# Three small moves in a four-layer image kernel: weight sums to GpSimd, statistics to another loop, a residual to ScalarE and GpSimd

## The chip, the cores and the metric

The kernel runs on one core of a Trainium2 chip. The metric is the device time of one execution in microseconds, the median of five runs. The core's engines are named as the profile names them: PE (TensorE, matmuls; PEld are its weight loads), DVE (VectorE), ACT (ScalarE), POOL (GpSimd) and SP (SyncE, which issues DMAs). L12 is line 12 of the kernel before.

## The reference

Eight images x of 512 channels by 32 x 32 pixels, in float32, go through four layers. Cut to what matters:

```python
# layer 0: group norm (8 groups), attention with 8 heads, three inner steps, projection
h = group_norm(x, scale, bias)
q, k, v = split(qkv_w @ h + qkv_b)
h = softmax(q.T k / 8) v                      # per head, 64 channels
for _ in range(3):
    h = h + 0.1 * tanh(inl_w @ h + inl_b)
x = x + proj_w @ h + proj_b
# layer 1: attention with one head of 64 channels for q and k, 512 for v
x = x + (Wv x + bv) softmax(q.T k).T
# layer 2: upsample by 2 with a 12-tap FIR, leaky relu, downsample by 2
x = down(leaky_relu(up(x + bias)) * sqrt(2))
# layer 3: a bottleneck whose weights are mixed from 8 experts for each image
rw = sigmoid(mean(x) @ router_w.T + router_b)
w1, w2, w3 = (sum(rw[e] * w[e] for e in range(8)) for w in (w1, w2, w3))
h = relu(bn(conv1x1(x, w1)))                  # 512 -> 128 channels
h = relu(bn(conv3x3(h, w2)))                  # 128 -> 128
x = relu(bn(conv1x1(h, w3)) + x)              # 128 -> 512
```

## The kernel before, in words

Channels lie on partitions in four blocks of 128; an image is a tile of 128 partitions by 4 x 1024. Layers 0, 1 and 2 run image by image, and the result of each image is spilled to device memory. Layer 3 then runs over all images. The instructions of each engine are put into a fixed order when the program is built, and the pools of buffers decide which tile waits for which: a step on an engine waits for everything ahead of it on that engine.

**Products.** The 512 x 512 projections (q, k, v, inl, proj, and v of layer 1) are computed as seven products of quarter matrices instead of eight (`product`). This needs sums of quarters of the weights (five for each matrix, `weight`, L339 to L343) and of the data (eight operations for each source, `quarter_sums`, L353 to L356; their tiles are named T_h, T_hf and T_x). The product's steps are named P1, C11 (both in the banks `_A`, from plain quarters of the data and of the weight), U2, U3, C21 (banks `_X`) and C22, C12 (banks `_Y`); of these U2, U3, C21 and C22 read data sums, and U2, U3, C22 and C12 read weight sums. For image 0 the weight quarters are loaded from the inputs, two of them into a tile `raw_`, and the five sums are made, for q on DVE and for k and v on POOL; POOL's queue then stores the seven parts (`stored`), and later images load them ready-made.

**Group norm.** `group_norm` takes the statistics of x (L278, L279: eight `bn_stats` and four `bn_aggr`), averages over groups with two tiny matmuls (gn_mean, gn_var) and writes h. In the program's text it stands at the head of layer 0. In the built order the statistics of image b+1, whose x is loaded early, run on DVE within the v product of layer 1 of image b.

**Layer 0's projection.** The residual x + proj is partly added by POOL (L523, three adds of the P1 term for each of two u), beside DVE's T_hf.

**Layer 1.** The v product is interleaved with the scores. Then a loop over eight blocks ic of 128 positions (the AV loop, L722 on) transposes x (xT), adds row_bias on DVE into a tile `y` (two buffers), multiplies by the attention, finishes y on DVE (L737), and writes it by DMA to a padded image, from which `halo` loads read overlapping tiles for layer 2.

**Layer 3.** `mixed(b)` forms the mixed weights of image b in a tile of two buffers, in five parts (w1e, three of w2e, w3e): each part is one product with the first expert's weight (L925) and seven multiply-adds (L927) on DVE. For image b, `c1` is a 1x1 product of z (16 matmul records), which ACT turns into `rim` (relu, batch norm, L942, one for each half g); `c2` is the 3x3 convolution of rim (36 records), which ACT turns into h2 (L958); `c3` is the last product (16 records, through two banks), whose eight results DVE scales and adds to z in place (L967), and ACT finishes with a relu (L970). In the built order, the c3 matmuls of image b alternate with c1 of image b+1.

Of the kernel before, what the change touches and what calls it, by code (L numbers as in the profile page):

```python
# [9 lines left out]
F32 = mybir.dt.float32  # L10
BF16 = mybir.dt.bfloat16
AF = mybir.ActivationFunctionType  # L12
ALU = mybir.AluOpType
# [4 lines left out]
P = 128  # L18
B, C, H, W = 8, 512, 32, 32
S = H * W  # L20
CC = C // P
# [31 lines left out]
def tile_sequence(ctx: ExitStack, tc: tile.TileContext, a: dict, out: bass.AP, shifted: bool):  # L53
# [213 lines left out]
                    ps[r], ones[HD * r : HD * r + 1, :], shift[r], start=False, stop=True  # L267
                )

    def group_norm(b, x):  # L270

        stats = tmp(f"stats_{b}", S)[:, 0 : CC * 2 * 6].rearrange(
            "p (c h s) -> p c h s", c=CC, h=2
        )
        mv = small.tile([P, CC, 2], F32, tag="mv", bufs=2, name=f"mv_{b}")
        for cc in range(CC):
            for h in range(2):
                nc.vector.bn_stats(stats[:, cc, h, :], x[:, cc, ts(h, HALF)])  # L278
            nc.vector.bn_aggr(mv[:, cc, :], stats[:, cc, :, :].rearrange("p h s -> p (h s)"))  # L279
        mean_c, var_c = mv[:, :, 0], mv[:, :, 1]  # L280
        ps = bank(ps_tp, f"gn_mean_{b}")
        nc.tensor.matmul(ps[:, 0:CC], group_mean, mean_c, start=True, stop=True)
        mean = small.tile([P, CC], F32, tag="gmean", bufs=2, name=f"gmean_{b}")
        nc.vector.tensor_copy(mean, ps[:, 0:CC])
        dev = small.tile([P, CC], F32, tag="gdev", bufs=2, name=f"gdev_{b}")
        nc.vector.tensor_sub(dev, mean_c, mean)
        nc.vector.tensor_mul(dev, dev, dev)
        nc.vector.tensor_add(dev, dev, var_c)
        ps = bank(ps_tp, f"gn_var_{b}")
        nc.tensor.matmul(ps[:, 0:CC], group_mean, dev, start=True, stop=True)  # L290
        mul = small.tile([P, CC], F32, tag="gmul", bufs=2, name=f"gmul_{b}")
        nc.scalar.activation(mul, ps[:, 0:CC], AF.Sqrt, bias=eps)
        nc.vector.reciprocal(mul, mul)
        nc.vector.tensor_mul(mul, mul, gn_scale)
        add = small.tile([P, CC], F32, tag="gadd", bufs=2, name=f"gadd_{b}")
        nc.vector.tensor_mul(add, mean, mul)
        nc.vector.tensor_sub(add, gn_bias, add)
        h = big_tile(f"h_{b}", [P, CC, S])
        for cc in range(CC):
            nc.vector.tensor_scalar(  # L300
                h[:, cc, :], x[:, cc, :], mul[:, cc : cc + 1], add[:, cc : cc + 1],
                ALU.mult, ALU.add,
            )
        return h
# [19 lines left out]
    def weight(key, b):  # L324
        t = wpool.tile([P, len(PARTS), 2, QR], F32, tag="w", name=f"w_{key}_{b}", bufs=3)
        if b:
            nc.sync.dma_start(t, stored[key])
            return t
        src = a["qkv_wT"][:, "qkv".index(key) * C :] if key in "qkv" else a[key + "_wT"]
        raw = tmp(f"raw_{key}", S).rearrange("p (a cc o) -> p a cc o", a=2, o=QR)  # L330
        a21, a22 = raw[:, 0], raw[:, 1]
        for dst, i, j in ((t[:, 0], 0, 0), (t[:, 1], 0, 1), (a21, 1, 0), (a22, 1, 1)):
            nc.sync.dma_start(
                dst, src[j * QR : j * QR + QR, i * QR : i * QR + QR].rearrange(
                    "(cc p) o -> p cc o", p=P
                )
            )
        eng = nc.vector if key == "q" else nc.gpsimd
        eng.tensor_add(t[:, 3], a21, a22)  # L339
        eng.tensor_sub(t[:, 4], t[:, 3], t[:, 0])  # L340
        eng.tensor_sub(t[:, 5], t[:, 0], a21)
        eng.tensor_sub(t[:, 6], t[:, 1], t[:, 4])
        eng.tensor_scalar(t[:, 2], a22, -1.0, None, ALU.mult)  # L343
        nc.gpsimd.dma_start(stored[key], t)
        return t

# [186 lines left out]

        return made

    def layer0(b, x, w):
        h = group_norm(b, x)
        t = quarter_sums(f"h_{b}", h)
        q = big_tile(f"q_{b}", [P, CC, S])
        k = big_tile(f"k_{b}", [P, CC, S])  # L540
# [92 lines left out]
        if b + 1 < B:  # L633
            w["k"] = weight("k", b + 1)

    def layer1(b, x, w):

        qk = big_tile(f"qk1_{b}", [P, S + HALF])
        q, k = qk[:, 0:S], qk[:, S : S + HALF].rearrange("d (p j) -> d p j", j=P)
# [82 lines left out]
        for ic in range(SC):  # L722
            ps = bank(ps_tp, f"xT_{b}_{ic}")
            for cc in range(CC):
                nc.tensor.transpose(ps[:, ts(cc, P)], x[:, cc, ts(ic, P)], ident)
            y = work.tile([P, C], F32, tag="y", name=f"y_{b}_{ic}", bufs=2)
            nc.vector.tensor_add(y, ps, row_bias)
            ps = bank(name=f"av1_{b}_{ic}")
            sh, u = divmod(ic, 4)
            for jc in range(SC):  # L730
                nc.tensor.matmul(  # L731
                    ps, eT[sh][:, jc, ts(u, P)], v[:, jc, :],
                    start=(jc == 0), stop=(jc == SC - 1),
                )
            if ic == 1:
                totals(1)
            nc.vector.scalar_tensor_tensor(y, ps, inv[:, ic : ic + 1], y, ALU.mult, ALU.add)  # L737
            for r in range(4):
                nc.scalar.dma_start(
                    ypad[b % 2][4 * ic + r + 3, 3 : W + 3, :], y[W * r : W * r + W, :]  # L740
                )
            if ic:
                halo.load(ic - 1)
        halo.load(NT - 1)
        halo.load_last()
        return halo
# [96 lines left out]
    with tc.tile_pool(name=f"weights_{run}", bufs=1) as wpool:  # L843
        w = {key: weight(key, 0) for key in ("q", "k", "v")}
        w["qk1"] = wpool.tile([P, CC, P], F32, name="w_qk1")
        for i, key in enumerate(("q1_wT", "k1_wT")):
            nc.sync.dma_start(
                w["qk1"][:, :, ts(i, HD)], a[key].rearrange("(cc p) o -> p cc o", p=P)
            )

        for b in range(B):
            x = x_next
            layer0(b, x, w)
            if b + 1 < B:
                x_next = load_x(b + 1)
            halo = layer1(b, x, w)
            layer2(b, halo)


# [58 lines left out]
    def mixed(b):  # L918
        wt = pool3.tile([P, WCOLS], F32, tag="mixed", name=f"mixed_{b}")
        parts = [(w1e, 0, C)]  # L920
        parts += [(w2e[ky], C + ky * 3 * P, 3 * P) for ky in range(3)]
        parts += [(w3e, C + 9 * P, C)]
        for src, at, n in parts:
            dst = wt[:, at : at + n]
            nc.vector.tensor_scalar_mul(dst, src[:, 0, :], rw[:, b, 0:1])  # L925
            for e in range(1, NE):
                nc.vector.scalar_tensor_tensor(  # L927
                    dst, src[:, e, :], rw[:, b, e : e + 1], dst, ALU.mult, ALU.add
                )
        return wt  # L930

    wt_next = mixed(0)
    for b in range(B):
        z, wt = z_next, wt_next
        if b + 1 < B:
            z_next = load_z(b + 1)
            wt_next = mixed(b + 1)
        h1 = rims[b % 2]
        for g in range(2):
            ps = bank(name=f"c1_{b}_{g}")  # L940
            project(ps, wt[:, 0:C].rearrange("p (cc o) -> p cc o", o=P), 0, z, g)
            nc.scalar.activation(  # L942
                h1[:, 1 + 16 * g : 17 + 16 * g, 1 : W + 1],
                ps.rearrange("p (h w) -> p h w", w=W),
                AF.Relu, bias=bn[0][1], scale=bn[0][0],
            )
        h2 = pool3.tile([P, S], F32, tag="h2", name=f"h2_{b}")
        for g in range(2):
            ps = bank(name=f"c2_{b}_{g}")
            for tap in range(9):  # L950
                ky, kx = divmod(tap, 3)
                nc.tensor.matmul(  # L952
                    ps.rearrange("p (h w) -> p h w", w=W),
                    wt[:, C + tap * P : C + (tap + 1) * P],
                    h1[:, ky + 16 * g : ky + 16 * g + 16, kx : kx + W],
                    start=(tap == 0), stop=(tap == 8),
                )
            nc.scalar.activation(  # L958
                h2[:, ts(g, HALF)], ps, AF.Relu, bias=bn[1][1], scale=bn[1][0]
            )  # L960
        for oc in range(CC):
            for g in range(2):
                ps = bank(ps_tp, f"c3_{b}_{oc}_{g}")
                at = C + 9 * P + oc * P
                nc.tensor.matmul(ps, wt[:, at : at + P], h2[:, ts(g, HALF)], start=True, stop=True)
                dst = z[:, oc, ts(g, HALF)]
                nc.vector.scalar_tensor_tensor(  # L967
                    dst, ps, bn[2][0][:, oc : oc + 1], dst, ALU.mult, ALU.add
                )
                nc.scalar.activation(dst, dst, AF.Relu, bias=bn[2][1][:, oc : oc + 1])  # L970
            nc.sync.dma_start(out[b, ts(oc, P), :], z[:, oc, :])

    if shifted:
# [80 lines left out]
```

## Time and profile before

| | |
|---|---|
| median of five runs | 4117.13 us (4112.2 to 4117.71) |
| profiled execution: time, span | 4118.64 us, 4116.4 us |
| granted TensorE clock over the span | 0.988 |
| busy over the span: PE, DVE, ACT, POOL | 97%, 59%, 26%, 13% |
| first matmul (gn_mean of image 0) | 28.70 us |
| PE's idle before proj_X, 16 times | 41.0 us |
| first matmul of layer 3's c1 | 3867.56 us |

Times are microseconds from the start of the span. The timeline's lines give start, duration, engine, line, operation, `out<-in`, the number of instructions that are merged, and in brackets the idle time before them with what ended it. The groups' lines give busy time, mean duration in ns, and the idle time before them. "PE x <- DVE y" among the waits is time in which PE stood idle until DVE's y was done. The table of windows gives for each stretch the busy time of PE, PEld, DVE, ACT and POOL with the number of their instructions, then the granted clock, the share of DMA, and GB/s.

### The profile page before, as it was taken

The numbers are of one execution on the slowest core, as the hardware profiler recorded it, in microseconds if no ns is written. First come the engines' busy times: TensorE is split into PE (matmuls) and PEld (weight loads), VectorE is DVE, ScalarE is ACT, GpSimd is POOL, SyncE is SP. The second block draws the span as 40 slices with busy tenths as digits, with TensorE's granted clock in tenths as the row PEclk, the third lists the DMA queues.
The fourth block names the chain that finished last, engine by engine and source line by source line (L and its number), as shares of the span: only waits on it lengthen the run. The fifth ranks groups of instructions, "written<-read, shape, count | busy, mean of one in ns | idle before, by whom it ended". The sixth has DMA issues, their size and how long they took to land.

```text
span 4116.4 us, 36926 instructions
## 1 busy us (share of the span) xinstructions
PE 3977.3 (97%) x14034; PEld 1923.2 (47%) x14034; DVE 2443.4 (59%) x3421; ACT 1080.3 (26%) x1478; POOL 521.1 (13%) x382
## 2 busy tenths in 40 slices
PE   6999999999999999999999999999999999999899
PEld 3334553355434463355434554355533554345543
DVE  4768448634676347754486346763477345763696
ACT  0431214112332114212241123322142123422123
POOL 3321003100121002110030002110031001201000
PEclk9999999999999999999999999999999999999899
DMA  4002310032001310023101310013100221003333
GB/s 176 24 16 77 111 64 1 39 100 78 36 1 56 121 57 19 1 92 106 54 1 56 105 55 36 1 71 112 69 1 39 83 79 52 1 0 115 147 153 124
DMA packets 85307, 259.98 MB, mean 63 GB/s; under 512 B 13958, under 2 KB 20102, under 8 KB 78336
## 3 DMA queue, kind: packets, MB, share of 16 engines
q1 hardware_dynamic: 69520, 227.31, 15.5%
q10 hardware_dynamic: 12960, 16.81, 1.5%
q0 software_dynamic: 2640, 13.40, 0.9%
q8 instruction: 113, 1.85, 0.2%
q14 instruction: 74, 0.61, 0.0%
HBM read 194.57 MB, written 62.91 MB: 63 GB/s over the span
## 4 chain that ended last, share of the span: by engine, by line
PE 84%; DVE 11%; ACT 2%; issue 1%; DMA 0%; SPq 0%; ACTq 0%; DVEq 0%
PE scores L263 12%; PE av L731 11%; PE av L595 10%; PE inl_X L389 6%; PE dn L819 6%; PE v_X L389 4%; PE inl_A L389 4%; PE inl_Y L389 4%; DVE up L778 3%; PE v_Y L389 3%; PE c L952 3%; PE proj_X L389 2%; PE q_X L389 2%; PE k_X L389 2%; PE v_A L389 2%; ACT leak L777 2%
## 5 line engine op out<-in xcount | busy, mean ns | idle before, releaser
L580 ACT ACTIVATE e<-scores 128x1024 f32<-128x1024 f32 x512 | 496.7, 1022 | 506.7 <-PE scores L263 504.2
L586 DVE TENSOR_TENSOR acc<-acc,e 128x1024 f32<-128x1024 f32 x384 | 493.7, 1286 | 116.3 <-ACT e L580 97.8
L263 PE MATMUL scores<-q,k 64*128 64x512 f32 x2048 | 511.3, 616 | 9.9 <-ACT e L580 6.6
L595 PE MATMUL av<-e,v 128*64 128x512 f32 x2048 | 494.1, 604 | 0.0
L731 PE MATMUL av<-v,eT 128*128 128x512 f32 x1024 | 450.1, 592 | 0.0
L612 POOL TENSOR_TENSOR seen<-seen,acc 128x512 f32<-128x512 f32 x128 | 206.9, 1616 | 1607.9 <-DVE acc L586 1602.9
L263 PEld LDWEIGHTS scores<-q,k 64*128 64x128 f32 x2048 | 175.2, 186 | 338.1 <-ACT e L580 167.2
L777 ACT ACTIVATE leak<-up 128x512 f32<-128x512 f32 (+1 forms) x264 | 147.9, 595 | 591.5 <-DMA ypad_u<-y 445.0
L731 PEld LDWEIGHTS av<-v,eT 128*128 128x128 f32 x1024 | 189.6, 190 | 214.3 <-issue 212.1
L595 PEld LDWEIGHTS av<-e,v 128*64 128x64 f32 x2048 | 124.9, 136 | 338.8 <-issue 336.5
L389 PE MATMUL inl_X<-T_hf,w_inl 128*128 128x512 f32 x576 | 262.0, 592 | 0.0
L737 DVE SCALAR_TENSOR_TENSOR y<-av,inv,y 128x512 f32<-128x512 f32 x64 | 48.0, 750 | 360.2 <-PE av L731 360.2
L819 PE MATMUL dn<-dn_op,up 128*128 128x126 f32 (+5 forms) x2048 | 235.8, 275 | 0.0
L819 PEld LDWEIGHTS dn<-dn_op,up 128*128 128x128 f32 (+1 forms) x2048 | 231.1, 192 | 8.8 <-DVE up L778 6.5
L793 PE MATMUL up<-halo,up_op 126*128 126x512 f32 x512 | 229.1, 600 | 1.4 <-DVE up L778 1.4
L609 DVE RECIPROCAL inv<-total 128x512 f32<-128x512 f32 x64 | 214.9, 3357 | 10.0 <-PE total L605 10.0
L778 DVE SCALAR_TENSOR_TENSOR up<-up,leak 128x512 f32<-128x512 f32 (+1 forms) x264 | 171.5, 686 | 76.1 <-ACT leak L777 71.1
L389 PE MATMUL inl_A<-hf,w_inl 128*128 128x512 f32 x384 | 175.6, 602 | 0.0
L612 POOL TENSOR_TENSOR seen<-seen,inv 128x512 f32<-128x512 f32 x64 | 125.4, 1960 | 388.3 <-DVE inv L609 388.3
L389 PEld LDWEIGHTS inl_X<-T_hf,w_inl 128*128 128x128 f32 x576 | 109.0, 190 | 139.0 <-issue 109.9
L793 PEld LDWEIGHTS up<-halo,up_op 126*128 126x128 f32 x512 | 93.5, 189 | 130.5 <-issue 65.6
L389 PE MATMUL proj_X<-T_hf,w_proj 128*128 128x512 f32 x192 | 110.5, 720 | 41.0 <-DVE T_hf L354 41.0
(251 smaller groups left out, 4933.5 us busy)
## 6 DMA issues: line engine op xcount, KB each, us to landing
halo<-ypad_u SPq DMA_DIRECT2D x256, 252.0 KB
w_v<-stored_u_v SPq DMA_DIRECT2D x14, 1792.0 KB
x<-in_x_dram SPq DMA_DIRECT2D x32, 512.0 KB
ypad_u<-y ACTq DMA_DIRECT2D x256, 64.0 KB
spill_u<-z SPq DMA_DIRECT2D x32, 512.0 KB
z<-spill_u SPq DMA_DIRECT2D x32, 512.0 KB
out_dram<-z SPq DMA_DIRECT2D x32, 512.0 KB
w_q<-stored_u_q SPq DMA_DIRECT2D x7, 1792.0 KB
```

The costliest lines, as they stand in the source:

```text
L263: nc.tensor.matmul(ps[r], k[r], q[r], start=True, stop=(shift is None))
L389: nc.tensor.matmul(dst, lhs, rhs, start=(opens and s == 0 and cc == 0), stop=(cc == 1 and s == rows), skip_group_check=True,)
L580: nc.scalar.activation(e, ps, AF.Exp, scale=HD ** -0.5)
L586: nc.vector.tensor_add(accs[g], accs[g], e)
L595: nc.tensor.matmul(avs[g][rows[r]], v[:, jc, ts(2 * oc + r, HD)], e[:, ts(r, HALF)], start=(jc == 0), stop=(jc == SC - 1),)
L609: nc.vector.reciprocal(inv, ps)
L612: nc.gpsimd.tensor_add(seen, seen, part)
L731: nc.tensor.matmul(ps, eT[sh][:, jc, ts(u, P)], v[:, jc, :], start=(jc == 0), stop=(jc == SC - 1),)
L777: nc.scalar.mul(t, ps, 0.2 * SQRT2)
L778: nc.vector.scalar_tensor_tensor(dst, ps, SQRT2, t, ALU.mult, ALU.max)
L793: nc.tensor.matmul(ps[i], up_op[0 : IR * IC, :], halo.tile(t)[0 : IR * IC, c + i, :], start=True, stop=True,)
L819: nc.tensor.matmul(rows[:, r0 - first : r1 + 1 - first, c0 : c1 + 1], up[t][0:k, c, ts(cc, P)], op[:, r0 - 4 * t + 3 : r1 + 4 - 4 * t, c0 ...
```

## The change

Three parts:

1. The five weight sums of q are made on POOL, as those of k and v were. 
2. The statistics move out of `group_norm` into `channel_stats`, with a buffer of the pool of `y`. For image 0 they stand ahead of layer 0; for image b+1 they are issued within layer 1 of image b, after block ic = 3 of the AV loop (`midway`).
3. In layer 3, the first product of each part of `mixed` is an ACT copy with a scale instead of a DVE product. For images 0 to 6 the c3 result is scaled and biased by ACT into a tile of its own (four buffers), POOL adds it to z, and ACT's relu no longer adds the bias. Image 7 keeps the DVE step.

In the built order of the changed program, DVE's statistics of image b+1 stand between the AV loop's fourth and fifth blocks, and for image 0 ahead of the row_bias add. On ACT in layer 3, the five first products of image b+2 stand between the relus of image b (the first of them ahead of the last relu) and the two rim steps of image b+1. PE's order is c3 of image b among c1 of image b+1 as before.

```diff
-    def group_norm(b, x):
-
-        stats = tmp(f"stats_{b}", S)[:, 0 : CC * 2 * 6].rearrange(
-            "p (c h s) -> p c h s", c=CC, h=2
-        )
+    def channel_stats(b, x):
+
+        stats = work.tile([P, C], F32, tag="y", name=f"stats_{b}", bufs=2)
+        stats = stats[:, 0 : CC * 2 * 6].rearrange("p (c h s) -> p c h s", c=CC, h=2)
         mv = small.tile([P, CC, 2], F32, tag="mv", bufs=2, name=f"mv_{b}")
         for cc in range(CC):
             for h in range(2):
                 nc.vector.bn_stats(stats[:, cc, h, :], x[:, cc, ts(h, HALF)])
             nc.vector.bn_aggr(mv[:, cc, :], stats[:, cc, :, :].rearrange("p h s -> p (h s)"))
+        return mv
+
+    def group_norm(b, x, mv):
...
-        eng = nc.vector if key == "q" else nc.gpsimd
-        eng.tensor_add(t[:, 3], a21, a22)
-        eng.tensor_sub(t[:, 4], t[:, 3], t[:, 0])
-        eng.tensor_sub(t[:, 5], t[:, 0], a21)
-        eng.tensor_sub(t[:, 6], t[:, 1], t[:, 4])
-        eng.tensor_scalar(t[:, 2], a22, -1.0, None, ALU.mult)
+        nc.gpsimd.tensor_add(t[:, 3], a21, a22)
+        nc.gpsimd.tensor_sub(t[:, 4], t[:, 3], t[:, 0])
+        nc.gpsimd.tensor_sub(t[:, 5], t[:, 0], a21)
+        nc.gpsimd.tensor_sub(t[:, 6], t[:, 1], t[:, 4])
+        nc.gpsimd.tensor_scalar(t[:, 2], a22, -1.0, None, ALU.mult)
         nc.gpsimd.dma_start(stored[key], t)
...
             if ic:
                 halo.load(ic - 1)
+            if ic == 3:
+                midway()
...
+        mv = [channel_stats(0, x_next)]
         for b in range(B):
             x = x_next
-            layer0(b, x, w)
+            layer0(b, x, mv[0], w)
             if b + 1 < B:
                 x_next = load_x(b + 1)
-            halo = layer1(b, x, w)
+
+            def midway():
+                if b + 1 < B:
+                    mv[0] = channel_stats(b + 1, x_next)
+
+            halo = layer1(b, x, w, midway)
             layer2(b, halo)
...
             dst = wt[:, at : at + n]
-            nc.vector.tensor_scalar_mul(dst, src[:, 0, :], rw[:, b, 0:1])
+            nc.scalar.activation(dst, src[:, 0, :], AF.Copy, scale=rw[:, b, 0:1])
...
                 dst = z[:, oc, ts(g, HALF)]
-                nc.vector.scalar_tensor_tensor(
-                    dst, ps, bn[2][0][:, oc : oc + 1], dst, ALU.mult, ALU.add
-                )
-                nc.scalar.activation(dst, dst, AF.Relu, bias=bn[2][1][:, oc : oc + 1])
+                factor, term = bn[2][0][:, oc : oc + 1], bn[2][1][:, oc : oc + 1]
+                if b + 1 < B:
+
+                    t = pool3.tile([P, HALF], F32, tag="c3", name=f"c3_{b}_{oc}_{g}", bufs=4)
+                    nc.scalar.activation(t, ps, AF.Identity, bias=term, scale=factor)
+                    nc.gpsimd.tensor_add(dst, t, dst)
+                    nc.scalar.activation(dst, dst, AF.Relu)
+                else:
+                    nc.vector.scalar_tensor_tensor(dst, ps, factor, dst, ALU.mult, ALU.add)
+                    nc.scalar.activation(dst, dst, AF.Relu, bias=term)
```

More of the change, by code (lines that the diff above doesn't have):

```diff
@@ L534, in residual, with layer0 @@
         return made
-    def layer0(b, x, w):
-        h = group_norm(b, x)
+    def layer0(b, x, mv, w):
+        h = group_norm(b, x, mv)
         t = quarter_sums(f"h_{b}", h)
@@ L634, in layer0, with layer1 @@
             w["k"] = weight("k", b + 1)
-    def layer1(b, x, w):
+    def layer1(b, x, w, midway):
         qk = big_tile(f"qk1_{b}", [P, S + HALF])
```

## The prediction

> **What bounds the kernel now.** I read the page's busy times first, then the idle time of TensorE by releaser, then the three places that the change touches in the timeline, and last the groups of layer 3.
>
> ```profile
> PE 3977.3 (97%) x14034; PEld 1923.2 (47%) x14034; DVE 2443.4 (59%) x3421; ACT 1080.3 (26%) x1478; POOL 521.1 (13%) x382
> ```
>
> ```profile
> PE proj_X L389 <- DVE T_hf L354: 41.0, 16, 3.9
> PE gn_mean L282 <- DVE mv L279: 28.7, 1, 28.7
> ```
>
> PE is busy 97% of the span, so a gain can come only from its few gaps (the waits in the second fence: total, times, longest, in us) and a loss only from new ones. The largest single gap is the start, 28.7 us before the first matmul. The start on DVE, POOL and PE:
>
> ```profile
> 17.50 0.69 DVE L340 TENSOR_TENSOR w_q<-w_q 128x512 f32<-128x512 f32 x1
> 18.83 1.28 DVE L278 BATCH_NORM_STATS2 stats<-x 128x6 f32<-128x512 f32 x2
> 20.03 4.58 DVE L123 TENSOR_TENSOR row_bias<-row_bias,bias 128x512 f32<-128x512 f32 x1
> 37.21 0.68 DVE L353 TENSOR_TENSOR T_h<-h 128x512 f32<-128x512 f32 x1
> ...
> 20.99 1.26 POOL L341 TENSOR_TENSOR w_k<-w_k,raw_k 128x512 f32<-128x512 f32 x1
> ...
> 35.17 9.86 PE L389 MATMUL q_A<-h,w_q 128*128 128x512 f32 x16 [2.01 <-DVE h L300]
> 44.87 3.60 PE L389 MATMUL q_X<-T_h,w_q 128*128 128x512 f32 x8
> ```
>
> DVE does w_q's sums first, then the statistics, though x has landed by 9.56 us. A DVE add that takes 0.69 alone takes 4.58 while POOL forms w_k's sums. The same pairing in the projection, and the busy times and clock of two stretches around the stall that it makes:
>
> ```profile
> 318.95 9.96 POOL L523 TENSOR_TENSOR x<-x,proj_P 128x512 f32<-128x512 f32 x6 [61.12 <-ACT proj_P L521]
> 322.71 1.74 DVE L355 TENSOR_TENSOR T_hf<-hf 128x512 f32<-128x512 f32 x1
> 329.99 0.68 DVE L355 TENSOR_TENSOR T_hf<-hf 128x512 f32<-128x512 f32 x1
> ```
>
> ```profile
> 324.00:327.00 3.00, 0.73 (x2) 0.49 (x3) 3.00 (x3) 0.00 (x0) 3.00 (x2) 1.00 1.03 422
> 327.00:334.00 7.00, 5.77 (x8) 1.99 (x7) 5.59 (x7) 0.00 (x0) 3.98 (x13) 0.53 0.22 66
> ```
>
> In the windows PEclk is the third number from the end: after 3 us with PE busy 0.73, the clock is 0.53 for the next 7. Half clock for about 6.8 us costs about 3.4. Each of the eight long projection stalls (3.35 to 3.88 us) is followed by such a stretch; none of the 1.33-us ones is.
>
> Layer 3, groups of four images (3938 to 4055 us):
>
> ```profile
> L952 PE MATMUL c<-rim,mixed 128*128 128x512 f32 x142 | 61.6, 592 | 0.0
> L927 DVE SCALAR_TENSOR_TENSOR mixed<-w2e,rw,mixed 128x384 f32<-128x384 f32 x85 | 47.6, 610 | 0.0
> L967 DVE SCALAR_TENSOR_TENSOR z<-c,g,z 128x512 f32<-128x512 f32 x34 | 25.3, 745 | 2.3 <-PE c L965 2.3
> L970 ACT ACTIVATE z<-z,b 128x512 f32<-128x512 f32 x34 | 24.5, 721 | 23.8 <-DVE z L967 23.8
> L942 ACT ACTIVATE rim<-c,b,g 128x512 f32<-128x512 f32 x7 | 5.4, 775 | 3.5 <-PE c L308 3.5
> ```
>
> PE never idles there (0.0): an image is 68 matmul records at 0.43, 29.4 us from one c2 to the next, and DVE is nearly as full (27.7 of 29). ACT has room, 8 us busy of 29.
>
> **Part 1, the start.** Removed from DVE: five sums of w_q (3.2 us) and, more important, their place ahead of the statistics. These now run as x lands (8 x 0.6, done about 11), the norm's small steps follow, and h (4 x 0.75) is ready about 17; q_A can start near 15.4 instead of 35.17, since its first quarters of w_q land at 14.33. But U2 (the q_X line) needs both w_q's sums, now POOL's first five operations from 16.5 (5 x 1.3, done about 23.5), and the sums T_h, which DVE makes after row_bias while POOL runs 15 operations in a row until about 40. With the projection's price, row_bias and six T_h take 7 x 1.75 = 12.3 from about 17.5, so U2 starts near 30, against 44.87: 15 earlier. PE then idles about 5 us between q_A and U2, which by the windows above costs one slow stretch, 3.4. I take -11. Bounds: without contention U2 waits for w_q's sums and q_A alone, near 26: -18. If every DVE operation waits as row_bias did (4.58), T_h is not done before POOL is, and U2 stands near 44: nothing gained, 0. I stay near the projection row, because it is the same T_h operation. w_k's and w_v's sums end some 5 us later; k starts after 50, so this is free. The load of inl's raw quarters waits for the slot that w_v's sums free; it is needed near 240.
>
> [...]
>
> **Part 2, the statistics.** They leave layer 1's value product, where DVE spends about 5.3 us on them (8 x 0.6 and 4 x 0.2), and go between two output blocks of the AV loop. There DVE is idle 5.96 of each 7.3 us, waiting for PE, so they hide; if that cover were gone, 5.3 per image would show. The next block's transposed copy comes about 3.6 us later than now, its bank is wanted 7 us later: nothing. Gain: from the first q/k matmul of layer 1 to the first AV transpose PE takes 42.02 in image 7, which has no statistics there, 42.74 in images 1 and 3 to 6, and 46.35 in image 2, where a slow stretch falls (clock 0.67 from 1340 to 1347). So 5 x 0.72 + 4.33 = 7.9; image 0 is filled by layer 2's constants, 0 to 1. I take -8 (bounds -4, if another image catches the slow stretch, and -9).
>
> **Part 3, layer 3, images 0 to 6.** DVE loses per image eight residuals (8 x 0.745) and five first products (about 0.45 each); that frees about 7 us on an engine which PE hides already: worth nothing in steady state. ACT gains eight Identity copies (no such row; taken as L942's, 0.775, a PSUM read with scale and bias; the lower bound is L777's 0.595) and five first products of image b+2 (no row; from 0.45, DVE's time for them, to 0.72, L970's; taken as 0.72 for 512 columns, 0.6 for 384). POOL gains eight adds (1.27 alone, 1.66 in the projection's six).
>
> What matters is ACT's order, which is fixed: all Identity and relu steps of image b, then the five first products, then rim of image b+1 (only the first of them, w1e's, precedes the last relu). c2 of image b+1 waits for rim. From the first c3 of image b, PE needs 16 c3 and 16 c1 records, 13.8 us, plus about 1.2 waiting for c3 banks (two of them, now freed by ACT, which alternates with relus that wait for POOL): ready at 15. ACT starts about 1.1 after that c3; operations overlap by some 0.08, so eight Identity are 5.6, eight relus 5.2, the products 2.9 and rim 0.8: 15.6; it also waits twice for a POOL add (2 x 1.3): 18.2. PE stalls 18.2 - 15 = 3.2, plus the 1.2: 4.4 per image. Six boundaries have products (of images 2 to 7), 6 x 4.4 = 26.4; the seventh has none and costs about 2: +28. Bounds: Identity, relu and products at their low ends shorten ACT's chain by about 3, leaving 7 x 1.6 = +11; adds at 1.66 lengthen it to +43. Image 7 keeps the old steps.
>
> Then the clock. A 3.2-us stall is just short of the projection's. Ahead of the slow stretches PE was mostly busy 0.15 to 0.34 of the 3.41 us (half of 6.8) before, by the trace's matmul records. If such a stretch decides, with the limit near a third busy, a stall of 3.2 leaves 2.2 idle in one of them in about two alignments of three: 6 x 0.64 x 3.4 = +13 (bounds 0 and 7 x 3.4 = +24).
>
> [...]
>
> Sum: -11 - 8 + 28 + 13 = +22 on the profiled 4118.64, 4140.6; the median of the five runs lies 1.5 lower: 4139.
>
> **Rivals.** (A) Faster: ACT keeps up. Its price list is at the low end, rim is ready before c1 ends, there is no slow stretch, and POOL leaves T_h alone at the start: -18 - 8 + 11 = -15, 4102. It decides from an ACT chain 3.2 us shorter than mine. For it: ACT is busy only 8 of 29 now; against it: the 0.775 of L942 and the POOL adds inside the chain. (B) No slow stretches, the rest as forecast: -19 + 28 = +9, 4126; with a little less stall this is no change. For it: 3.2 is below every stall seen to throttle (3.35 and more). (C) POOL binds: adds take 1.66 beside DVE's mixing, layer 3 +43, stalls of about 5 throttle at every image (+24), start and statistics -19: +48, 4165. Against it: DVE mixes image b+2 only after c3 of b has freed its slot, so the two overlap little after image 1. (D) The start starves (0 instead of -11), the rest as forecast: +33, 4150. For it: the 4.58 row.
>
> **How the numbers follow.** About 0.2% (8 us) can be told from no change. Chances: forecast 0.42, D 0.16, C 0.12, B 0.16 (half of it within 8 us), A 0.14. With the tails of the forecast: faster 0.15, same 0.13, slower 0.72. The range leaves out half of C and the best of A: 4106 to 4162.
>
> **What would show it.** Right: q_A near 15 with U2 near 30 and T_h at 1.7; layer 1 at 42.0 in images 1 to 6; in layer 3 an idle of about 3 before c2, released by ACT rim, after three to five first products on ACT, a period near 34, and clocks of 0.5 after some of these stalls. Wrong: layer 3's period still 29.5 (then A), no clock below 1 there (B), adds at 1.6 (C), U2 beyond 40 (D).

## The result, and the profile after

The changed kernel takes 4122.45 us (median of 28 runs, 4115.35 to 4135.4) against 4115.63 for the kernel before, measured again beside it (48 runs, 4111.61 to 4119.06). The ratio is 1.0023, 95% interval 1.0018 to 1.0028: slower by 6.8 us in the medians (9.5 in the means), where 22 were forecast. The profiled execution took 4129.19 us (span 4127.3), so it is one of the slower ones.

The page's busy times:

```profile
PE 3986.6 (97%) x14034; PEld 1922.7 (47%) x14034; DVE 2403.8 (58%) x3320; ACT 1135.0 (28%) x1574; POOL 606.5 (15%) x443
```

and TensorE's idle time by releaser:

```profile
PE proj_X L390 <- DVE T_hf L355: 41.1, 16, 3.9
...
PE c L961 <- ACT rim L951: 12.6, 6, 2.5
PE gn_mean L284 <- DVE mv L278: 11.3, 1, 11.3
...
PE q_X L390 <- DVE T_h L355: 6.6, 1, 6.6
PE c L974 <- ACT c L980: 6.0, 1, 6.0
```

The gap at the start shrank from 28.7 to 11.3. Three waits are new: T_h at the start (6.6), rim ahead of c2 in layer 3 (six times, up to 2.5 us each), and one of 6.0 for a c3 bank in layer 3. The start in the timeline:

```profile
18.35 1.75 DVE L123 TENSOR_TENSOR row_bias<-row_bias,bias 128x512 f32<-128x512 f32 x1
20.02 1.75 DVE L354 TENSOR_TENSOR T_h<-h 128x512 f32<-128x512 f32 x1
...
26.65 4.96 DVE L355 TENSOR_TENSOR T_h<-h,T_h 128x512 f32<-128x512 f32 x1
...
15.36 8.80 PE L390 MATMUL q_A<-h,w_q 128*128 128x512 f32 x16 [2.00 <-DVE h L302]
24.00 1.02 PE L390 MATMUL q_X<-T_h,w_q 128*128 128x512 f32 x2
31.67 4.89 PE L390 MATMUL q_X<-T_h,w_q 128*128 128x512 f32 x6 [6.65 <-DVE T_h L355]
```

q_A starts at 15.36, and all but two records of U2 stand until 31.67 behind a T_h that took 4.96 beside POOL. Layer 3, the groups of 3950 to 4060 us:

```profile
L961 PE MATMUL c<-rim,mixed 128*128 128x512 f32 x108 | 52.2, 647 | 7.4 <-ACT rim L951 7.4
L981 POOL TENSOR_TENSOR z<-c,z 128x512 f32<-128x512 f32 x29 | 36.3, 1272 | 74.9 <-ACT c L980 74.9
...
L980 ACT ACTIVATE c<-c,b,g 128x512 f32<-128x512 f32 x28 | 21.1, 766 | 1.3 <-PE c L974 1.1
L982 ACT ACTIVATE z<-z 128x512 f32<-128x512 f32 x28 | 17.6, 630 | 7.0 <-POOL z L981 6.3
```

PE now idles before c2 (7.4 in three images; 0.0 before). One boundary, on PE and on ACT:

```profile
3952.40 5.31 PE L310 MATMUL c<-z,mixed 128*128 128x512 f32 x12
3960.16 17.42 PE L961 MATMUL c<-rim,mixed 128*128 128x512 f32 x36 [2.45 <-ACT rim L951]
...
3957.21 1.61 ACT L934 ACTIVATE mixed<-w2e,rw 128x384 f32<-128x384 f32 x3
3958.73 0.71 ACT L934 ACTIVATE mixed<-w3e,rw 128x512 f32<-128x512 f32 x1
3959.34 1.43 ACT L951 ACTIVATE rim<-c,b,g 128x512 f32<-128x512 f32 x2
```

c1 ended at 3957.7, and ACT made four first products of a later image before it came to rim. c2's 36 records take 17.42 instead of 15.62. The same place in windows (third number from the end: granted clock) shows why:

```profile
3957.70:3961.10 3.40, 0.95 (x3) 0.49 (x3) 3.40 (x7) 3.08 (x6) 0.00 (x0) 1.00 0.45 164
3961.10:3964.60 3.50, 3.50 (x6) 1.41 (x5) 3.50 (x7) 0.00 (x0) 0.00 (x0) 0.51 0.98 345
```

The slow stretch is there as forecast, but it lasts 3.4 us, not 6.8. And the first boundary, where image 0's residual begins:

```profile
3870.77 8.89 POOL L981 TENSOR_TENSOR z<-c,z 128x512 f32<-128x512 f32 x2 [156.90 <-ACT c L980]
```

Two adds that take 2.5 us elsewhere took 8.89: POOL stood beside DVE's unbroken multiply-adds of image 1's weights, and PE idled 5.95 us waiting for a c3 bank. The first of the two adds took 7.66 us by itself, the second 1.26.

### The profile page after: what moved, and what is told of

It reads as the page before. It is cut to its first block, busy times and chain, and to the rows that moved or that the text cites. A ratio compares the mean times of both kernels' runs of the same rounds, so it can differ in the third digit from the quotient of the medians.

```text
span 4127.3 us, 37015 instructions
## 1 busy us (share of the span) xinstructions
PE 3986.6 (97%) x14034; PEld 1922.7 (47%) x14034; DVE 2403.8 (58%) x3320; ACT 1135.0 (28%) x1574; POOL 606.5 (15%) x443
## 4 chain that ended last, share of the span: by engine, by line
PE 83%; DVE 11%; ACT 4%; issue 2%; POOL 1%; DMA 0%; ACTq 0%; SPq 0%; DVEq 0%
PE scores L263 12%; PE av L732 11%; PE av L596 10%; PE inl_X L390 6%; PE dn L822 6%; PE inl_A L390 4%; PE v_X L390 4%; PE inl_Y L390 4%; PE c L961 3%; DVE up L781 3%; PE v_Y L390 3%; PE proj_X L390 2%; PE q_X L390 2%; PE k_X L390 2%; PE v_A L390 2%; ACT leak L780 2%
## 5 line engine op out<-in xcount | busy, mean ns | idle before, releaser
L524 POOL TENSOR_TENSOR x<-x,proj_P 128x512 f32<-128x512 f32 x48 | 79.7, 1691 | 554.0 <-ACT proj_P L522 554.0
```

## The experiments

Every ratio is to the kernel before, run on the same chip. "Period" is the time from one image's c2 to the next.

### Part 1 alone

The five lines of the weight sums; nothing else.

> The kernel before with part 1 alone (the five sums of w_q on POOL). Here the built order puts row_bias, which waits for its DMA, between the statistics of image 0, so they end later than in the changed kernel. Theory 1 (taking w_q's sums from DVE's head is what brought the start forward): U2 near 33 to 36 us instead of 44.87, time about 4106 against 4115.6. Rival (the gain at the start came from the statistics' new place in part 2, and POOL's fifteen sums starve T_h): U2 beyond 41, time within 4 us of before.

Measured: 4112.78 us, ratio 0.9997 (0.9988 to 1.0006). U2 started at 44.82 and the first k matmul at 62.04, as before: the rival was right that this alone does not bring U2 forward. DVE in the timeline:

```profile
28.74 9.24 DVE L300 TENSOR_SCALAR h<-x,gmul,gadd 128x1024 f32<-128x1024 f32 x4
```

h took 9.24 beside POOL's sums (2.98 in the kernel before), so what DVE saved it lost again.

### Part 2 alone

`channel_stats`, its buffer and `midway`; the sums of w_q stay on DVE.

> The kernel before with part 2 alone (statistics in channel_stats, buffer from the pool of y, within the AV loop; w_q's sums stay on DVE, but the built order has image 0's statistics ahead of them). Theory 1: the start stays near that of before (U2 near 44), only layer 1 gains 0.7 per image and the attention phase of layer 0 0.7 per image, with one slow clock stretch of image 2 gone: about -12, 4103. Rival (the order of image 0's statistics ahead of w_q's sums makes the start's gain, not POOL): U2 near 30, and the time is about 4092, as low as with both parts.

Measured: 4097.46 us, ratio 0.9962 (0.9948 to 0.9975). The first k matmul stands at 54.16, 7.9 earlier; in images 2 to 7 the attention phase (first k matmul to first inl matmul) takes 179.1 us instead of 179.8, and in layer 1 the stretch of part 2's forecast takes 42.0, both as forecast here. At the start the rival is nearer: the order of image 0's statistics makes most of the gain there (7.9 of the 11.8 us of the changed kernel), although most of U2 waited until 34.93 for T_h. The time lies between the two forecasts, 4103 and 4092.

### Part 3 alone

Layer 3's edits only.

> The kernel before with part 3 alone (layer 3). Theory: layer 3 is longer by about 25 us of stalls (the first boundary, c2 of image 0 to c2 of image 1, by 15, because a POOL add of image 0 stands 7 us beside DVE's multiply-adds; then 3.2 per image, of which 2.4 is idle before c2), and by 0 to 10 more, according to how many of the boundaries are followed by a slow clock stretch: 4140 to 4150, with a wide spread of the single runs. Rival (the changed kernel's layer 3 costs only what its median shows beside parts 1 and 2 as forecast, some 26): 4142 with a spread no wider than before.

Measured: 4148.57 us (4144.21 to 4148.65), ratio 1.0079 (1.0065 to 1.0093), +32.7. From c2 of image 0 to c2 of image 7 it took 241.7 us (208.6 before); single periods were 32.9 without and 34.3 to 34.5 with a slow stretch; the first was 40.4. The spread was not wide.

### Parts 1 and 2 without part 3

> The changed kernel with the layer 3 of before, so parts 1 and 2 alone. Theory: in the profiles these two parts bring 24 us by the start of layer 3 (11.7 at the start, the rest in layer 1, the attention phase and one slow clock stretch), so the time is near 4092, faster than both kernels. Rival (the gains of the two parts are partly luck of the clock in one profiled execution): near 4100, with a spread like the changed kernel's.

Measured: 4092.21 us (4089.37 to 4095.03), ratio 0.9943 (0.9929 to 0.9957): -23.6, faster than both kernels. The first k matmul is at 50.0, so POOL's sums are worth another 4 us once the statistics come first. So layer 3 costs the changed kernel 4122.45 - 4092.21 = 30.2 in the medians, and about 33 by the two ratios, which go by the means.

### The statistics' buffer

To the kernel of the last run:

```diff
-        stats = work.tile([P, C], F32, tag="y", name=f"stats_{b}", bufs=2)
+        stats = tmp(f"stats_{b}", S)
```

> Parts 1 and 2 with the layer 3 of before, as in the run that reached 4092, but the statistics' buffer comes from the ring of four (tmp) again, not from the pool of y; their place in the program stays. Theory (the buffer decides what moved outside layer 1): ScalarE's load of the table for exp again waits for the first scores, so the attention phase of images 2 to 7 is 179.8 instead of 179.1, 4.3 in all; and in the built order row_bias again stands between image 0's statistics, so the start is as late as with part 1 alone (first k matmul near 62). Layer 1 stays at 42.0. Time near 4105. Rival (the place of the statistics decides): attention 179.1, start near 50, time near 4092.

Measured: 4112.47 us, ratio 0.9996 (0.9987 to 1.0005). This one line is worth 20 of the 24 us. The attention phase is back at 179.8 and the first k matmul at 61.04, as expected. What I had not expected: layer 1 is back at 42.73 too. With a free buffer in the ring of four, the built order puts the statistics into layer 1's value product again, although the program's text has them in the AV loop; a buffer of y's ring cannot be had before y is done with it. In the changed kernel the statistics wait for just that, the write of a y:

```profile
887.69 1.88 DVE L277 BATCH_NORM_STATS2 stats<-x 128x6 f32<-128x512 f32 x3 [2.59 <-DMA ypad_u<-y]
```

The attention phase is ScalarE's load of the table for exp (1.28 us). In the kernel before it waits for the first scores:

```profile
1068.61 1.28 ACT L580 ACT_TABLE_LOAD   x1 [41.75 <-PE scores L263]
```

and in the changed kernel only for DVE, long before them (the scores begin at 1054.97):

```profile
1042.63 1.28 ACT L581 ACT_TABLE_LOAD   x1 [28.21 <-DVE v_U L464]
```

In the built order the load waits for DVE and PE before, and for DVE alone after; the exp behind it then waits for PE. That the rotation of the ring, from which e also comes, decides which wait the load carries is the likely reason; shown is that the buffer's line switches it.

### Image 0's residual on DVE

```diff
-                if b + 1 < B:
+                if 0 < b < B - 1:
```

> The changed kernel, but image 0's residual in layer 3 stays on DVE as before. Theory: the 39.4 us from c2 of image 0 to c2 of image 1 come from a POOL add that DVE's multiply-adds for image 1 shut out for 7 us; without it that stretch is back near 24.5, the next one grows to about 36, because DVE starts image 2's weights later, and the sum of the two falls from 72.3 to about 61: time about 4111. Rival (the wait moves: DVE's extra 6 us make image 2's weights late, and the sum of the two stretches stays above 68): time about 4119.

Measured: 4117.96 us, ratio 1.0006 (0.9997 to 1.0015). The first two periods are 29.0 and 38.3, in sum 67.3 instead of 72.3. So image 0's residual on ACT and POOL made the 39.4, but of the 10.4 us that the first period lost, 5.4 came back in the second, nearer to the rival. Now image 1's adds stand beside DVE:

```profile
3899.14 11.76 POOL L981 TENSOR_TENSOR z<-c,z 128x512 f32<-128x512 f32 x6 [187.63 <-ACT c L980]
3900.67 9.10 DVE L936 SCALAR_TENSOR_TENSOR mixed<-w3e,rw,mixed 128x512 f32<-128x512 f32 x6
```

The first of these six adds took 3.40, the other five 1.71 each, in turn with DVE's multiply-adds (1.64 each, 0.75 alone). At image 0's boundary in the changed kernel DVE alternated between two mixes, w2e and w3e, each multiply-add begun before the last had ended, and the add beside it took 7.66. Here DVE works on w3e alone, each step on the result of the last, and the two engines take turns. No run tests whether this is what decides.

### First products back on DVE

The `nc.scalar.activation(... AF.Copy ...)` in `mixed` becomes `tensor_scalar_mul` on DVE again.

> The changed kernel with the first products of mixed back on DVE; the residual stays on ACT and POOL. Theory (the five products ahead of rim on ACT make the idle before c2): 2.8 us leave ACT's chain, more than the 2.45 of idle, so the period of images 2 to 6 falls from 32.7 (34.5 with a slow stretch) to about 30.2, with no slow stretch in layer 3; the first boundary keeps its 39. Time about 4107. Rival (the alternation of Identity, POOL's add and relu is what makes rim late): an idle of 1 us or more stays before c2 and the time is 4115 or more.

Measured: 4118.26 us (4113.99 to 4129.83), ratio 1.0012 (1.0002 to 1.0022). The period fell to 32.0 to 32.4, with no slow stretch after the first boundary, but 1.08 us of idle before c2 stayed, so the rival holds:

```profile
L981 POOL TENSOR_TENSOR z<-c,z 128x512 f32<-128x512 f32 x31 | 45.1, 1476 | 82.1 <-ACT c L980 82.1
```

The adds are slower (1476 ns, 1272 in the changed kernel). In the changed kernel DVE's multiply-adds cannot begin before ACT has made the products, after the adds; here they run beside them, and the relus wait.

### The w3e product alone back on DVE

```diff
+            if src is w3e:
+                nc.vector.tensor_scalar_mul(dst, src[:, 0, :], rw[:, b, 0:1])
+            else:
+                nc.scalar.activation(dst, src[:, 0, :], AF.Copy, scale=rw[:, b, 0:1])
```

> The changed kernel with only the w3e product of mixed back on DVE; ACT keeps the four others. Theory: idle before c2 falls by the product's 0.6 to about 1.8; a 3.41-us stretch then keeps PE busy for nearly half, so no slow stretch follows any boundary; period 32.2 for images 2 to 6, time about 4115, and single runs spread less. Rival (slow stretches do not depend on the length of the idle): slow stretches stay and the time falls by no more than 4.

Measured: 4126.86 us, ratio 1.0027 (1.0017 to 1.0037). Both theories missed: the idle grew to 2.66, with the slow stretches as before.

```profile
L984 POOL TENSOR_TENSOR z<-c,z 128x512 f32<-128x512 f32 x26 | 35.8, 1396 | 71.2 <-ACT c L983 71.2
```

ACT lost a product of 0.71, and its last waits for POOL grew from 1.31 to 2.13 (0.60, 1.09 and 0.44 at one boundary); POOL's adds took 1396 ns, which fits DVE starting on w3e beside them again, the mechanism of the run before at a smaller dose. The time cannot be told from the changed kernel's.

### The residual back on DVE

Layer 3 of before, but with the first products on ACT.

> The changed kernel with the residual back on DVE for all images; the first products of mixed stay on ACT. Theory (the products alone are hidden on ACT, since rim then waits for at most a few of them, and DVE gains 2.2 us per image, which PE covers but for the first two images): layer 3 as before or up to 3 us shorter, time 4089 to 4093. Rival (the products stand ahead of rim of the next image here too and delay it): an idle of 1 to 2 us before c2, period about 31, time about 4102.

Measured: 4087.52 us (4087.36 to 4097.67), ratio 0.9937 (0.9924 to 0.9951), the fastest version run. Periods are 29.0, 31.3 and then 29.5 to 29.6: the products are hidden on ACT. From parts 1 and 2 alone (4092.21) it cannot be told apart.

### The bias with the relu

```diff
-                    nc.scalar.activation(t, ps, AF.Identity, bias=term, scale=factor)
+                    nc.scalar.activation(t, ps, AF.Identity, scale=factor)
...
-                    nc.scalar.activation(dst, dst, AF.Relu)
+                    nc.scalar.activation(dst, dst, AF.Relu, bias=term)
```

> The changed kernel, but the bias of the last batch norm stays with ACT's relu (as in the kernel before) instead of going to the Identity step. Theory (the forecast's ACT chain was too long because the relu without bias takes 0.63 us and not the 0.72 of the row with bias): the relus are back at 0.72, ACT's chain is about 0.7 longer, idle before c2 grows from 2.45 to about 3.1, the period without a slow stretch from 32.9 to 33.6, time about 4127 to 4130. Rival (the relus lie in ACT's waits for POOL, so their length does not count): idle stays at 2.45 and the time at 4122.

Measured: 4114.81 us (4107.58 to 4118.33), ratio 0.9999 (0.999 to 1.0008). A clear miss: idle fell to 0.82, period 31.8, no slow stretch after the first boundary.

```profile
4012.53 15.72 PE L961 MATMUL c<-rim,mixed 128*128 128x512 f32 x36 [0.82 <-ACT rim L951]
```

The relus are back at 0.721 and the Identity steps fell from 0.766 to 0.673, so ACT's work stays nearly the same; but the built order changed as well. Identity and relu now alternate to the end, where the changed kernel waits for POOL twice:

```profile
3952.76 0.63 ACT L982 ACTIVATE z<-z 128x512 f32<-128x512 f32 x1 [0.60 <-POOL z L981]
3953.30 1.43 ACT L980 ACTIVATE c<-c,b,g 128x512 f32<-128x512 f32 x2
3955.44 0.63 ACT L982 ACTIVATE z<-z 128x512 f32<-128x512 f32 x1 [0.71 <-POOL z L981]
```

These two waits, 1.31 of the 1.63 by which the idle fell, are the likely reason. Order and prices changed together here, so it is not shown; shown is that the relu's price does not add up to the idle.

### The products made twice

```diff
             nc.scalar.activation(dst, src[:, 0, :], AF.Copy, scale=rw[:, b, 0:1])
+            nc.scalar.activation(dst, src[:, 0, :], AF.Copy, scale=rw[:, b, 0:1])
```

> The changed kernel with each first product of mixed made twice on ACT, so the chain ahead of rim is about 2.8 us longer. Theory: idle before c2 is about 5.2, and every one of the boundaries is followed by a slow stretch. If what counts is how much of the stretch is left when PE starts again, its cost is between 1.7 and 3.4 us, and the period is 37.1 to 38.8; time 4145 to 4155. Rival (by the forecast's price, a whole 6.8-us slow stretch is paid after each stall, 3.4): period at the upper end, 38.8 or more, time 4155 or more.

Measured: 4150.68 us, ratio 1.0084 (1.007 to 1.0098). Idle 5.20, period 37.6 to 38.2, within the theory's range: what was paid is what is left of the slow stretch when PE starts. The windows:

```profile
4003.40:4006.80 3.40, 0.67 (x2) 0.00 (x0) 2.42 (x4) 3.40 (x8) 0.00 (x0) 1.00 0.38 154
4006.80:4010.20 3.40, 0.93 (x1) 0.50 (x2) 3.40 (x7) 3.08 (x6) 0.00 (x0) 0.50 0.83 300
4010.20:4013.60 3.40, 3.40 (x5) 1.35 (x4) 3.40 (x8) 0.00 (x0) 0.00 (x0) 0.50 0.80 305
```

In the first slow stretch PE is busy 0.93 of 3.40, and a second follows; most of the first lies in the stall and adds nothing to it, and c2 takes 17.86, 2.2 more than the 15.62 at full clock.

### rim ahead of the products

`wt_next = mixed(b + 1)` moves from the head of image b to behind its c2.

> The changed kernel with mixed(b+1) called after image b's c2 instead of at the head of image b; in the built order, rim of the first half then stands ahead of four of the five products on ACT, rim of the second half behind them. Theory (the order on ACT makes the idle before c2): idle falls from 2.45 to below 0.5 us, since the first half of c2 needs rim's second half only in its last taps; period about 30.5, no slow stretch in layer 3, first boundary still 39: time about 4107. Rival (rim's second half holds c2 up as before): period 32 or more, time 4117 or more.

Measured: 4116.0 us (4107.72 to 4118.74), ratio 0.9997 (0.9988 to 1.0006). Idle before c2 fell to 0.32 and no slow stretch followed the later boundaries, so the order on ACT is what makes both; but the period is 31.7, not 30.5, since c3 waits about 0.4 and 0.5 for its banks at two places while POOL's adds take 1418 ns beside DVE.

### The changed kernel, three more profiles

> The changed kernel, profiled once more. Theory (single executions of it lie between 4115 and 4135 because a slow stretch follows some, all or none of layer 3's boundaries): the periods of images 2 to 6 are each 32.9 without a slow stretch and 34.4 with one, their number differs from one profile to the next, and the time follows that number by about 1.6 us each, together with slow stretches in the layers before. Rival (something else spreads the times): layer 3 takes the same time in each profile.

> As the run before it: a third profile of the changed kernel, for the number of slow stretches in layer 3 and the time that goes with it.

> As the two runs before it: a fourth profile of the changed kernel.

Measured: 4122.79, 4121.86 and 4129.99 us. Layer 3 from c2 of image 0 to c2 of image 7 took 241.8, 241.4 and 239.2 (242.4 in the first profile), with four, four and three slow stretches after the first boundary (five there). So their number differs, as the theory said, but by 3 us in all, and the slowest of the three has the fewest. What makes it slow lies elsewhere:

```profile
1651.10:1654.50 3.40, 1.67 (x7) 0.49 (x6) 2.05 (x3) 0.00 (x0) 1.27 (x1) 1.00 0.00 0
1654.50:1657.90 3.40, 3.40 (x5) 1.33 (x4) 3.37 (x2) 0.42 (x1) 1.40 (x2) 0.51 0.00 0
```

In images 3 to 7 of that profile (4129.99) a slow stretch follows the short waits (1.73 in image 3) between attention and the inner steps, and that phase takes 73.99 instead of 72.38, five times 1.6. In the profile of 4122.79 no image has this.

## Why the prediction was wrong

The direction held, and so did the mechanism of layer 3: rim comes late behind ACT's work, PE stalls (2.45), and half clock follows (granted clock 0.51). The size did not: 22 were forecast and 6.8 measured. The step that failed most is the price of a slow stretch in part 3, taken as 3.4 us from the projection, where 1.5 to 1.8 were measured. Next come parts 1 and 2, which brought 23.6 where I had 19, and last the stalls of layer 3, about 26 where I had 28.

- **Part 1 (-11).** The sum of the start is right, 62.04 to 50.26 for the first k matmul, 11.8, and U2 near 30 (31.67). That it is right is partly luck: of the seven DVE operations ahead of U2, which I took as 1.75 each, one took 0.68, one 1.09 and one 4.96. The cause is wrong. I put the gain down to the weight sums, but part 1 alone gives nothing, and part 2 alone 7.9. I had read the order of the changed program as that of part 1.
- **DVE and POOL beside each other.** T_h at 1.75 came as priced. The price did not cover the T_h of 4.96, during which three whole POOL adds passed (1.28, 1.28 and 1.27), nor the POOL add of 7.66 (1.27 alone), during which ten of DVE's multiply-adds passed (0.61 and 0.75 each). No run shows what decides between a short and a long wait.
- **Part 2 (-8).** Layer 1's 42.0 came as said, 0.72 in five images. The 4.33 of image 2 was in the profile of before (4118.64, 3 above the later median), and is not in the profiles of the kernels with part 1 alone or the old buffer; it should not have been counted whole against a median. Missing was the table load: 0.71 in each of images 2 to 7, 4.3 in all. In medians both parts bring 23.6, where I had 19. The start (11.8), layer 1 (3.6) and the table load (4.3) make 19.7 of it; the other 3.9 are not placed.
- **Part 3, stalls (+28).** The profile's 242.4 less 208.6 is 33.8; without five slow stretches at 1.6 that is +26, close, but made up otherwise. The steady idle is 2.45 and not 3.2, and the period 32.9 and not 33.8. From the first c3 to rim ACT takes 17.2, where I had 18.2. Two terms of that sum were too large: the relu without a bias takes 0.63, and I took 0.72 from the row with one, eight times 0.09; and ACT waits about 1.8 per image for POOL (6.3 for 28 relus), where I had 2.6. What each is worth is open: with the bias back on the relu the idle fell instead of growing. The first period is 15.1 longer than before (39.4 against 24.3), 10.4 of it through image 0's residual on ACT and POOL, with the add of 7.66 beside DVE; the second is 2.3 shorter (32.9 against 35.1). I had put that contention in rival C and argued it away "after image 1"; it is image 0 where it fell.
- **Part 3, clock (+13).** The term that was most out of size, by its price and not by its count: I had 6 x 0.64, about four stretches, and three to five came (beside the one of the first boundary, which lies in its 15.1). I took 3.4 for each slow stretch from the projection, where a stall of 1.23 lies in the slow stretch and half clock lasts 6.8 us (327.42 to 334.24 in image 0). Here PE starts before or as the slow stretch begins and is busy all through it, and full clock is back after one: 3.4 us at half clock, 1.5 to 1.8 each. Three to five of them make +5 to +8. The limit that I supposed, near a third busy, was my estimate and is not shown: half clock also followed a stretch with PE busy 1.67 of 3.40.
- **Rivals.** B's number, 4126, is nearest, for the wrong reason: slow stretches are there, and cheaper. A fails on ACT's order, C on the adds' steady 1272 ns, D on U2 at 31.67, though its starvation shows in part 1 alone.

Added up: parts 1 and 2 were 4.6 better than forecast in medians. Layer 3 cost 30.2 in medians, about 33 by the ratios and 30.6 to 33.8 in the four profiles of the changed kernel, where I had 41. Of these 7 to 11 us the clock is 5 to 8 and the stalls about 2.

## What to carry to other kernels

Before an effect is put down to an edit, look in the built order for what else moved: here the ring that a small buffer comes from decided where the statistics ran and what a table load waited for, 20 us for one line. Work moved to an idle engine is priced by its place in that engine's fixed order, ahead of whose input it stands, and not by the idle share. Here GpSimd's adds took 1.27 us where VectorE's multiply-adds came after them, and 1.42 to 1.48 on average in two runs where they ran beside them, 7.66 at worst in the changed kernel; a product that delays VectorE past the adds can be worth keeping where it is.

## What the runs showed of the hardware

- Half clock followed short stalls here: in the changed kernel after 3.4 us with PE busy 0.95 (2.45 of idle), in the last of its further profiles after 3.4 us with PE busy 1.67, between attention and the inner steps. In the first of them 3.4 us with PE busy 1.08 (2.45 of idle) had full clock behind it. Stalls of 0.32 (rim ahead of the products), 0.82 (bias with the relu) and 1.08 (first products on DVE) had none in layer 3 after the first boundary: c2 took 15.72 there. The slow stretches keep a grid: in the trace of the changed kernel they begin at 3927.01, 3961.15, 3995.28, 4029.41 and 4063.55 us, ten stretches of 3.41 apart, and the period there, 34.46, is nearly the same, so that one boundary after another was hit.
- These five lasted one stretch of 3.41 us each, with PE busy all through. So did the one at the first boundary (from 3879.23), with PE busy 2.83; with 5.20 of idle (the products made twice) PE was busy 0.93 of the first 3.40 and a second followed. c2 took 1.5 to 2.2 us longer, about half of the time that PE worked at half clock. Through the router's 64 matmuls of 8 columns the profile calls PE busy all the time, and the clock stayed at half for their 13.8 us.

```profile
3824.60:3828.00 3.40, 3.40 (x18) 3.40 (x17) 0.85 (x2) 0.00 (x0) 0.00 (x0) 0.50 1.00 428
```

- Beside long runs of the other engine, both VectorE (4.96 for 0.68, three adds of GpSimd) and GpSimd (7.66 for 1.27, ten multiply-adds of VectorE) waited through several instructions in the changed kernel; with image 0's residual on DVE the two took turns (1.71 for 1.27 beside 1.64 for 0.75).
